# Order of transposes, squares and a small product around matmuls in halves, in a two-layer graph network on one core

## The chip, the core and the metric

The kernel runs on one core of a Trainium2 chip. The metric is the device time of one execution in microseconds (us). The core has five engines that matter here: TensorE (PE in the profile; its weight loads are PEld), VectorE (DVE), ScalarE (ACT), GpSimd (POOL) and SyncE (SP), which here issues nearly all transfers. Each works through its own list of instructions in order and waits for the others through semaphores.

## The reference

For each of 16 batches there are 1024 nodes with 128 features (`x`) and a 1024 x 1024 matrix `adj`. A first network adds a gathered, degree-scaled and weighted sum to `x` and normalises each node. A second network has four layers with both directions of the matrix, each normalised by the root of its sums of squares. All of it is in float32.

```python
def _L0_gnn_ref(embeddings, adjacency_matrix, cost_matrix, W, b):
    degree = adjacency_matrix.sum(axis=-1)[:, :, None]
    sum_neighbors = jnp.einsum('bid,bij->bjd', embeddings, cost_matrix) / degree
    concatenated = jnp.concatenate([embeddings, sum_neighbors], axis=-1)
    return jax.nn.relu(jnp.einsum('bnk,dk->bnd', concatenated, W) + b)

def _l2norm(x, axis):
    n = jnp.sqrt(jnp.sum(x * x, axis=axis, keepdims=True))
    return x / jnp.maximum(n, EPS)

def _layer(nodes, adj, ws, bs, wd, bd, wn, bn, wu, bu):
    src_agg = jnp.einsum('bjv,bij->biv', nodes @ ws + bs, _l2norm(adj, 2))
    dst_agg = jnp.einsum('bjv,bji->biv', nodes @ wd + bd, _l2norm(adj, 1))
    upd = jnp.concatenate([src_agg, nodes @ wn + bn, dst_agg], axis=2)
    return jnp.tanh(upd @ wu + bu)
# four such layers with kept inputs concatenated, then:
x = _layernorm(x + _L0_gnn_ref(x, adj, adj, L0_gnn_W, L0_gnn_b), axis=-1)
x = _layernorm(x + _L1_gnn_ref(x, adj, ...), axis=-1)
```

## The kernel before

The kernel works through the batches in turn. In the layers of batch `b` it already prepares batch `n = b + 1`: its degrees, its sums of squares by rows and columns, its scaling, its first network (`first_gnn`) and the transposed matrix `at`. Layers are numbered from 0, so "layer two" of the change's name is layer 1 in the code.

`aggregate` multiplies messages with quarters of the matrix in a Winograd form: seven products in place of eight, with combined quarters `T` (of `a`) and `Q` (of `at`). Two matmuls, in the upper and the lower half of the array's columns, are issued as a pair. A dictionary of `hooks` says at which pair other engines' work (and a few small products) enter the instruction lists.

```python
def transpose_rows(st, q, at):
    h, o = divmod(q * QB * C, HW)
    n = QB // len(st)
    for j in range(0, NB, NJ):
        for i, piece in enumerate(st):
            c = slice(o + i * n * C, o + (i + 1) * n * C)
            nc.vector.transpose(
                at[h][:, j:j + NJ, c].rearrange("p j (k c) -> p j k c", c=C),
                piece.rearrange("p k (j c) -> p j k c", c=C)[:, j:j + NJ])
...
def combine(i, y, T):
    if i == 2:
        nc.vector.tensor_sub(T[2], y[1, 1], y[0, 1])
    elif i == 3:
        nc.vector.tensor_sub(T[3], T[2], y[0, 0])
    else:
        nc.vector.tensor_sub(T[4], y[1, 0], T[2])
...
def degree_of(a, state, i, engine=nc.scalar):          # ScalarE, sum of a row
    ...
    nc.scalar.activation(a[:, i, :], a[:, i, :], AF.Copy, accum_out=degree)

def squares_of_row(n, a, state, i):                     # ScalarE
    sq = two.tile([P, N], F32, tag="sq", ...)           # two buffers
    nc.scalar.activation(sq, a[:, i, :], AF.Square, accum_out=state["cols"][:, i:i + 1])
    state[i] = sq

def add_squares(b, state, i):                           # VectorE
    ...
    nc.vector.tensor_add(state["acc"], state["acc"], state[i])

def column_sums(b, state):                              # VectorE: transpose, then reduce to `part`
    column_reduce(b, state, column_transpose(b, state))

def inverses(b, state, first=0):
    cols = state["cols"]
    pc = small(f"pc{b}")
    by_halves(pc, fold, state["part"])                  # TensorE: the column sums' product
    own = ...
    nc.vector.tensor_mul(own, pc..., group...)
    nc.vector.reduce_sum(cols[:, NB:2 * NB]..., own..., axis=AX.X)
    root_inverses(cols, state["inv"], slice(first, 2 * NB))   # VectorE max, GpSimd power
```

In layer 0 of every batch but the first, the rest of `at` is transposed from rows that ScalarE has scaled. Quarter 0 of the rows arrives in two pieces, in the buffers `xa` and `acc`; quarter 1 in two pieces in `sq` buffers.

```python
def rows3():
    for q in (1, 0):
        transpose_rows(rows[q], q, at)
hooks = {0: rows3, 3: lambda: combine(4, y, T), 5: lambda: combine_1(yt), 7: lambda: combine(2, yt, Q),
         9: lambda: combine(3, yt, Q), 11: lambda: combine(4, yt, Q), 17: sums1, 28: first_addition}
aggregate(b, 0, feats, t, a, at, T, Q, f1, "row", hooks)
```

In layer 1, at fixed pairs of `aggregate`, reads of the accumulators (`m1_read`, `m3_half`, `m4_read`, `m2_and_half_of_m3`, `last_reads`) are issued as well, the last at pair 22; the layer ends with an addition on VectorE and a tanh on ScalarE:

```python
for i, pair in enumerate(zip(up, lo)):
    if i - 2 * n in events:
        events[i - 2 * n]()
    if i in hooks:
        hooks[i]()
    for o, x, y, start, stop in pair:
        nc.tensor.matmul(o, x, y, start=start, stop=stop)
nc.vector.tensor_add(e0, e0, Z0)
squash(l, 0, e0, fT)
```

Then `messages` of layer 2 begins, with VectorE additions of the products `pt`; behind the first of them `factors` takes the result of `inverses`, and sends the column factors through memory to `cinv`, by which VectorE scales the next matrix (`a<-a,cinv`).

Of the kernel before, what the change touches and what calls it, by code (L numbers as in the profile page):

```python
# [23 lines left out]
def adj_resnorm_kernel(ctx: ExitStack, tc: tile.TileContext, x, adj, w0, b0, layers, out):  # L24
# [35 lines left out]
    NB = N // P  # L60
# [8 lines left out]
    NJ = NB // 2  # L69
# [107 lines left out]
    def small(name, shape=(K,)):  # L177
        return ps_s.tile([P, *shape], F32, tag="small", name=name)

    def by_halves(out, x, y, start=True, stop=True):  # L180

        for s in (slice(V, P), slice(V)):
            nc.tensor.matmul(out[s], x[:, s], y, start=start, stop=stop)  # L183
# [53 lines left out]
    def begin_sums(b):  # L237
        cols = two.tile([P, 3 * NB], F32, tag="cols", name=f"cols{b}")
        inv = two.tile([P, C], F32, tag="inv", name=f"inv{b}")
        nc.gpsimd.memset(inv[:, 3 * NB:], 0.0)  # L240
        return {"cols": cols, "inv": inv}
# [22 lines left out]
    def column_sums(b, state):  # L264

        column_reduce(b, state, column_transpose(b, state))

    def column_transpose(b, state):
        tr = two.tile([P, N], F32, tag="sq", name=f"acct{b}")
        nc.vector.transpose(tr, state["acc"])  # L270
        return tr

    def column_reduce(b, state, tr):
        part = two.tile([P, K], F32, tag="part", name=f"part{b}")
        nc.vector.reduce_sum(part, tr.rearrange("p (k r) -> p k r", r=C), axis=AX.X)
        state["part"] = part
# [16 lines left out]
# [4 lines that stand above are left out]
        by_halves(pc, fold, state["part"])  # L297
        own = one.tile([P, NH, G, BPH], F32, tag="own", name=f"own{b}")
        nc.vector.tensor_mul(own, pc.rearrange("p (h g k) -> p h g k", h=NH, g=G),
                             group[:, None, :, None].to_broadcast([P, NH, G, BPH]))  # L300
        nc.vector.reduce_sum(cols[:, NB:2 * NB].rearrange("p (h k) -> p h k", h=NH),
                             own.rearrange("p h g k -> p h k g"), axis=AX.X)
        root_inverses(cols, state["inv"], slice(first, 2 * NB))

    def root_inverses(cols, inv, s):
        nc.vector.tensor_scalar_max(cols[:, s], cols[:, s], NORM_EPS * NORM_EPS)
        nc.gpsimd.tensor_tensor(inv[:, s], cols[:, s], mhalf[:, s], ALU.pow)
# [115 lines left out]
    def summed(name, tag):  # L423
        return one.tile([P, K, C], F32, tag=tag, name=name)
# [127 lines left out]
    def scale_rows(st, q, rinv):  # L552
        n = QB // len(st)
        for k in range(QB):
            row = st[k // n][:, k % n]
            nc.scalar.activation(row, row, AF.Copy, scale=rinv[:, q * QB + k:q * QB + k + 1])

    def transpose_rows(st, q, at):
        h, o = divmod(q * QB * C, HW)
        n = QB // len(st)  # L560
        for j in range(0, NB, NJ):
            for i, piece in enumerate(st):
                c = slice(o + i * n * C, o + (i + 1) * n * C)
                nc.vector.transpose(  # L564
                    at[h][:, j:j + NJ, c].rearrange("p j (k c) -> p j k c", c=C),
                    piece.rearrange("p k (j c) -> p j k c", c=C)[:, j:j + NJ])
# [4 lines left out]
    def quarters(a):  # L571
        return {(j, h): a[:, j * NJ:(j + 1) * NJ, half(h)] for j in range(2) for h in range(NH)}

    def quarters_t(at):
        return {(j, h): at[h][:, j * NJ:(j + 1) * NJ] for j in range(2) for h in range(NH)}

    def combined(b, kind):

        return {i: one.tile([P, NJ, HW], F32, tag=f"{kind}{i}", name=f"{kind}{i}_{b}") for i in (2, 3, 4)}

    def combine_1(y):

        nc.vector.tensor_sub(y[0, 1], y[0, 1], y[0, 0])  # L583
# [8 lines that stand above are left out]
# [203 lines left out]
    FIRST, LAST, ALL = range(BPH), range(BPH, NB), range(NB)  # L795
# [32 lines left out]
    Q = combined(0, "Q")  # L828
# [166 lines left out]
    for b in range(B):  # L995
        nxt = b + 1 < B
        n = b + 1
        y, yt = quarters(a), quarters_t(at)
        st = {}
# [4 lines left out]
        if b == 0:  # L1004
# [25 lines left out]
            def fold_and_scale(l, q):  # L1030
                fold_begin(l, fetched[l])
                scale_rows(rows[q], q, rinv)
# [16 lines left out]
            def folded(l, part):  # L1049
                return lambda *_: part(l, fetched[l])  # L1050

            hooks = {4: lambda *_: inverses(0, st0, NB), 5: folded(2, fold_begin), 6: rows0, 7: cinv0,
                     8: folded(2, fold_end), 9: lambda *_: fold_and_scale(3, 0), 11: second0, 12: folded(3, fold_end),
                     14: lambda *_: scale_rows(rows[1], 1, rinv), 18: first0, 26: sums0}
            T = combined(0, "T")
# [4 lines left out]
        else:  # L1060
            w = {}
            if nxt:
                w["a"] = load(n)
                st = begin_sums(n)
            t = messages(b, 0, feats, wm)
            wm = message_weights(b, 1)
            Q = combined(b, "Q")
# [12 lines left out]
            def first_addition(st=st):  # L1080
                if nxt:
                    add_squares(n, st, 1)

            hooks = {0: rows3, 3: lambda: combine(4, y, T), 5: lambda: combine_1(yt), 7: lambda: combine(2, yt, Q),
                     9: lambda: combine(3, yt, Q), 11: lambda: combine(4, yt, Q), 17: sums1, 28: first_addition}
# [9 lines left out]
        def sums_of(*rows, of=(), engine=nc.scalar, add=()):  # L1095

            def issue():
                for i in of:
                    degree_of(a2, st, i, engine)
                for i in rows:  # L1100
                    squares_of_row(n, a2, st, i)
                for i in add:
                    add_squares(n, st, i)
            return issue

        hooks = {}
        if b == 0:
            hooks = {0: sums_of(0, 1, add=(1,)), 1: lambda: combine(2, yt, Q), 2: sums_of(2, 3, add=(2, 3)),
                     3: lambda: combine(3, yt, Q), 4: sums_of(4, 5, of=(0, 1), add=(4, 5)), 5: lambda: combine(4, y, T),
                     11: sums_of(of=(2, 3)), 13: sums_of(6, 7, of=(4,)), 15: sums_of(of=(5,)),  # L1110
                     18: lambda: combine(4, yt, Q), 19: sums_of(of=(6, 7), add=(6, 7)), 27: lambda: column_sums(n, st)}
            st = begin_sums(n)
        else:
            nm = f"1_{b - 1}"
            w = {"ys": summed(f"y{nm}", "xa")}
            sums_of_next = {}
            if nxt:
                sums_of_next = {1: sums_of(2, 3, add=(2,)), 2: sums_of(of=(2, 3, 4, 5)), 8: sums_of(4), 10: sums_of(add=(3,)),
                                12: sums_of(5, add=(4,)), 15: sums_of(6, add=(5,)), 19: sums_of(7, add=(6,)),
                                20: sums_of(of=(6,)), 21: sums_of(add=(7,)), 23: sums_of(of=(7,)),  # L1120
                                24: lambda: column_sums(n, st), 29: lambda: inverses(n, st)}

            def begin1(w=w, nm=nm):
                norm_spread(w["ys"], f4, KS)
                w["s"] = norm_sum(w["ys"], KS, nm, back)

            def centre1(w=w, nm=nm):
                w["sq"] = norm_centre(w["ys"], w["s"], KS, nm)
                if nxt:
                    w["xs"] = load_spread(n)  # L1130

            def squares1(w=w, nm=nm):
                w["v"] = norm_squares(w["sq"], KS, nm)

            def rstd1(w=w, nm=nm):
                w["r"] = norm_rstd(w["v"], KS, nm)

            hooks = {0: begin1, 11: centre1, 14: squares1, 18: rstd1, **sums_of_next}
        aggregate(b, 1, feats, t, a, at, T, Q, f23, "row", hooks)
        if b:  # L1140
            second_norm, xs2 = w, w.get("xs")


        feats = [(f1, 1), (f23, 0)]
# [42 lines left out]
        hooks, between = {4: end1} if b else {}, {}  # L1187
        if nxt:
            scales = [lambda: scale(0, 1), lambda: scale(NJ, 1), lambda: scale(0, 0), lambda: scale(NJ, 0)]
            if b == 0:  # L1190
                between = {1: inverses3, 3: factors}
                hooks = {1: load_xn, 5: factors_of_rows, 7: start3, 18: factors_gathered,
                         **dict(zip((10, 12, 14, 16), scales))}
                quarters_at = (20, 22, 25)
            else:
                between = {0: factors, 1: end1_and_load}
                hooks = {2: factors_of_rows, **dict(zip((4, 5, 7, 9), scales)), 10: factors_gathered, 16: start3}
# [12 lines left out]
        hooks, between = {}, {}  # L1210
        if nxt:
# [64 lines left out]
            hooks = {0: squares0, 7: rstd0, 10: rows0, 14: end0, 18: quarters0, 23: rows1, 27: rows2}  # L1276
        else:
# [14 lines left out]
            hooks = {30: residual_last, 31: transpose_last}  # L1292
# [5 lines left out]
        if nxt:  # L1298
# [4 lines left out]
            T = w["T"]  # L1303
# [52 lines left out]
```

## Time and profile before

| what | value |
|---|---|
| time, median of 3 runs | 2435.02 us (2433.85 to 2435.8) |
| span of the profiled run | 2438.5 us |
| TensorE busy | 2415.8 us, 99% |
| TensorE weight loads busy | 1058.5 us, 43% |
| VectorE busy | 1909.6 us, 78% |
| ScalarE busy | 957.1 us, 39% |
| matmul of 128x512 (one of a pair) | 592 to 597 ns |
| VectorE transpose of a split piece, 128x512 | 669 to 695 ns |
| VectorE addition of squares, 128x1024 | 1221 ns |
| ScalarE square of a row block, 128x1024 | 1048 ns |

A line of the timeline has the start in us from the span's start, the length in us, the engine, the line of the kernel, the operation and the tiles (out <- in); in brackets stands how long the engine was idle before it and what ended that. The list of waits gives the same idle times in sums. Matmuls overlap in the records, and their ends are modelled, so a stop of TensorE is best seen in the distance between starts.

### The profile page before, as it was taken

The page shows a single profiled execution, that of the slowest core. Times are in us where ns is not written, and L with a number is a line of the kernel's source. Part 1 is how long each engine was busy: PE and PEld are TensorE (multiplying, and loading weights), DVE is VectorE, ACT ScalarE, POOL GpSimd, SP SyncE. Part 2 cuts the span into 40 slices and gives each one's busy share as a digit, 9 for nine tenths or more (in the row PEclk, how much of TensorE's full clock was granted, in tenths as well). Part 3 has the DMA queues.
Part 4 walks back from the last instruction along what each step waited for, and adds up shares of the span by engine and source line. Part 5 has one row for each costly group of instructions (what it writes and reads, how often), then busy time and mean ns, then how long its engine had stood idle before and what let it go on. Part 6 is the DMA issues. An engine that isn't in the chain of part 4 may idle for free.

```text
span 2438.5 us, 34361 instructions
## 1 busy us (share of the span) xinstructions
PE 2415.8 (99%) x13245; PEld 1058.5 (43%) x13245; DVE 1909.6 (78%) x2495; ACT 957.1 (39%) x1794; POOL 287.1 (12%) x100
## 2 busy tenths in 40 slices
PE   8999999999999999999999999999999999999998
PEld 5433444444444344443444435444443444434433
DVE  5878878798787978869788787887878878798743
ACT  5415334263342624425244351533515334262321
POOL 4101111101111011110011110111100111101100
PEclk9999999999999999999999999999999999999999
DMA  9517254261633517245172352624427254261410
GB/s 207 108 48 150 53 113 90 66 135 44 135 80 73 116 44 156 62 88 101 45 160 59 83 106 58 142 59 99 94 63 140 52 121 93 63 126 44 96 24 9
DMA packets 365732, 219.92 MB, mean 90 GB/s; under 512 B 152769, under 2 KB 336833, under 8 KB 365569
## 3 DMA queue, kind: packets, MB, share of 16 engines
q1 hardware_dynamic: 364800, 215.36, 41.8%
q0 software_dynamic: 768, 2.36, 0.3%
q8 instruction: 105, 1.72, 0.3%
q14 instruction: 59, 0.48, 0.1%
HBM read 199.17 MB, written 18.46 MB: 89 GB/s over the span
## 4 chain that ended last, share of the span: by engine, by line
PE 78%; DMA 9%; DVE 8%; SPq 2%; issue 2%; ACT 1%; DVEq 0%; ACTq 0%; POOLq 0%
PE m L773 33%; PE z L773 20%; PE pt L183 14%; PE m_f L516 5%; DMA a<-in_adj_dram 5%; PE z_f L516 2%; PE pw L183 2%; DMA rows<-in_adj_dram 2%; DVE at L564 2%; SPq L549 2%; DMA rows_acc<-in_adj_dram 1%; DVE Q L587 1%; DVE at L583 1%; DVE T L591 1%; DMA raw<-in_L_gnn_ws_dram 1%
## 5 line engine op out<-in xcount | busy, mean ns | idle before, releaser
L773 PE MATMUL m<-Q,S 128*64 128x512 f32 x1008 | 445.4, 593 | 3.1 <-DVE Q L587 2.9
L387 POOL TENSOR_TENSOR rs<-ve,mhalf 128x32 f32<-128x32 f32 x30 | 205.2, 6839 | 1955.9 <-DVE ve L385 1955.9
L773 PE MATMUL m<-at,t 128*64 128x512 f32 x1008 | 395.3, 594 | 0.3 <-DVE at L564 0.3
L773 PE MATMUL m<-T,S 128*64 128x512 f32 x1008 | 394.9, 593 | 0.0
L773 PE MATMUL m<-a,t 128*64 128x512 f32 x1008 | 392.8, 593 | 0.0
L607 DVE TENSOR_TENSOR t<-pt,wm 128x512 f32<-128x512 f32 x256 | 175.2, 689 | 159.6 <-PE pt L183 159.5
L773 PEld LDWEIGHTS m<-Q,S 128*64 128x64 f32 x1008 | 135.6, 137 | 275.2 <-issue 259.7
L773 PE MATMUL z<-Q,t 128*64 128x512 f32 x504 | 231.0, 597 | 2.0 <-DVE Q L591 2.0
L686 ACT COPY e<-m 64x512 f32<-64x512 f32 x63 | 36.6, 580 | 496.5 <-PE m L773 496.1
L773 PE MATMUL z<-a,t 128*64 128x512 f32 x504 | 231.2, 597 | 0.0
L773 PE MATMUL z<-a,S 128*64 128x512 f32 x504 | 227.1, 593 | 0.0
L773 PE MATMUL z<-at,S 128*64 128x512 f32 x504 | 226.7, 592 | 0.0
L773 PE MATMUL z<-at,t 128*64 128x512 f32 x504 | 226.6, 592 | 0.0
L183 PE MATMUL pt<-wm,f1T 128*64 128x256 f32 x1536 | 219.4, 380 | 0.0
L773 PEld LDWEIGHTS m<-T,S 128*64 128x64 f32 x1008 | 122.1, 137 | 130.1 <-issue 128.2
L773 PEld LDWEIGHTS m<-at,t 128*64 128x64 f32 x1008 | 119.8, 137 | 130.5 <-issue 127.0
L773 PEld LDWEIGHTS m<-a,t 128*64 128x64 f32 x1008 | 121.1, 137 | 122.8 <-issue 119.5
L773 PE MATMUL z<-T,t 128*64 128x512 f32 x384 | 172.8, 592 | 0.0
L345 DVE TENSOR_TENSOR a<-a,cinv 128x512 f32<-128x512 f32 x250 | 154.2, 691 | 12.8 <-DMA cinv<-dr 9.1
L183 PE MATMUL pt<-wm,f23T 128*64 128x256 f32 x1024 | 160.5, 379 | 0.0
L253 ACT ACTIVATE sq<-a 128x1024 f32<-128x1024 f32 x120 | 125.7, 1048 | 69.6 <-DVE acc L262 61.5
L183 PEld LDWEIGHTS pt<-wm,f1T 128*64 128x64 f32 x1536 | 121.7, 137 | 58.4 <-ACT f1T L786 12.0
(238 smaller groups left out, 4278.1 us busy)
## 6 DMA issues: line engine op xcount, KB each, us to landing
a<-in_adj_dram SPq DMA_DIRECT2D x120, 512.0 KB, 11.3
a<-in_adj_dram SPq DMA_DIRECT2D x240, 128.0 KB, 4.4
rows<-in_adj_dram SPq DMA_DIRECT2D x240, 64.0 KB, 3.0
wm<-wsave SPq DMA_DIRECT2D x16, 512.0 KB, 4.7
xn<-in_x_dram SPq DMA_DIRECT2D x124, 64.0 KB, 2.0
wm<-wsave SPq DMA_DIRECT2D x31, 256.0 KB, 3.7
xs<-in_x_dram SPq DMA_DIRECT2D x60, 128.0 KB, 3.6
cinv<-dr SPq DMA_DIRECT2D x30, 256.0 KB, 5.3
```

The costliest lines, as they stand in the source:

```text
L183: nc.tensor.matmul(out[s], x[:, s], y, start=start, stop=stop)
L253: nc.scalar.activation(sq, a[:, i, :], AF.Square, accum_out=state["cols"][:, i:i + 1])
L345: engine.tensor_mul(a[:, i, s], a[:, i, s], cinv[:, s])
L387: nc.gpsimd.tensor_tensor(rstd, ve, mhalf[:, :n], ALU.pow)
L516: nc.tensor.matmul(o, x_, y_, start=start, stop=stop)
L549: queue.dma_start(piece[g * C:(g + 1) * C, :, h * P:(h + 1) * P], v[h, g, :, i * n:(i + 1) * n])
L564: nc.vector.transpose(at[h][:, j:j + NJ, c].rearrange("p j (k c) -> p j k c", c=C), piece.rearrange("p k (j c) -> p j k c", c=C)[:, j:j + NJ])
L583: nc.vector.tensor_sub(y[0, 1], y[0, 1], y[0, 0])
L587: nc.vector.tensor_sub(T[2], y[1, 1], y[0, 1])
L607: nc.vector.tensor_add(t[j][:, o:o + 2].rearrange("p k a v c -> p k (a v c)"), pt, wm[:, 0][:, None, :].to_broadcast([P, 2, 2 * P]))
L686: nc.scalar.copy(e0[high], A[high])
L773: nc.tensor.matmul(o, x, y, start=start, stop=stop)
```

## The change

Four things are done, and no operation is added or taken away. First, `transpose_rows` goes through a split quarter of rows piece by piece, so that both transposes of the first piece stand ahead of those of the second. Second, in every middle batch the small product of the column sums (`inverses`) is issued behind the last matmul of layer 1 instead of ahead of its last pair. Third, squares and their additions for the next matrix take other places in layer 1 of the middle batches. Fourth, in layer 1 of the first batch the degrees of the first four row blocks come early, those of the last four late, and the last two additions come behind the last reads of the accumulators. The aim is that TensorE does not have to wait for VectorE's and ScalarE's side work.

```diff
     def transpose_rows(st, q, at):
         h, o = divmod(q * QB * C, HW)
         n = QB // len(st)
-        for j in range(0, NB, NJ):
-            for i, piece in enumerate(st):
+        for i, piece in enumerate(st):
+            for j in range(0, NB, NJ):
                 c = slice(o + i * n * C, o + (i + 1) * n * C)
                 nc.vector.transpose(
...
         if b == 0:
-            hooks = {0: sums_of(0, 1, add=(1,)), 1: lambda: combine(2, yt, Q), 2: sums_of(2, 3, add=(2, 3)),
-                     3: lambda: combine(3, yt, Q), 4: sums_of(4, 5, of=(0, 1), add=(4, 5)), 5: lambda: combine(4, y, T),
-                     11: sums_of(of=(2, 3)), 13: sums_of(6, 7, of=(4,)), 15: sums_of(of=(5,)),
-                     18: lambda: combine(4, yt, Q), 19: sums_of(of=(6, 7), add=(6, 7)), 27: lambda: column_sums(n, st)}
+            hooks = {0: sums_of(0, 1, add=(1,)), 1: lambda: combine(2, yt, Q), 2: sums_of(of=FIRST),
+                     3: sums_of(2, 3, add=(2, 3)), 4: lambda: combine(3, yt, Q), 5: sums_of(4, 5, add=(4, 5)),
+                     6: lambda: combine(4, y, T), 13: sums_of(6, 7), 18: lambda: combine(4, yt, Q), 19: sums_of(of=LAST),
+                     22: sums_of(add=(6, 7)), 27: lambda: column_sums(n, st)}
...
                 sums_of_next = {1: sums_of(2, 3, add=(2,)), 2: sums_of(of=(2, 3, 4, 5)), 8: sums_of(4), 10: sums_of(add=(3,)),
-                                12: sums_of(5, add=(4,)), 15: sums_of(6, add=(5,)), 19: sums_of(7, add=(6,)),
-                                20: sums_of(of=(6,)), 21: sums_of(add=(7,)), 23: sums_of(of=(7,)),
-                                24: lambda: column_sums(n, st), 29: lambda: inverses(n, st)}
+                                12: sums_of(5, add=(4,)), 13: sums_of(6), 15: sums_of(add=(5,)),
+                                17: sums_of(add=(6,)), 19: sums_of(7), 20: sums_of(of=(6,)), 21: sums_of(add=(7,)),
+                                23: sums_of(of=(7,)), 24: lambda: column_sums(n, st)}
...
         aggregate(b, 1, feats, t, a, at, T, Q, f23, "row", hooks)
         if b:
             second_norm, xs2 = w, w.get("xs")
+            if nxt:
+                inverses(n, st)
```

`sums_of(rows, of, add)` issues the degrees `of`, the squares of `rows` and the additions `add`; `FIRST` and `LAST` are the first and last four row blocks.

## Prediction

> **What bounds the kernel now.** I read the page's first parts, then who waited for whom on TensorE, then the timeline of each place where TensorE's matmuls start late. The page first, the busy times and the row of the granted clock:
>
> ```profile
> PE 2415.8 (99%) x13245; PEld 1058.5 (43%) x13245; DVE 1909.6 (78%) x2495; ACT 957.1 (39%) x1794; POOL 287.1 (12%) x100
> ...
> PEclk9999999999999999999999999999999999999999
> ```
>
> TensorE is never without work for long, at full clock, and the change takes no matmul away. So the most the change can give is the time in which TensorE stands still. Who waited for whom, TensorE alone (total us, times, longest):
>
> ```profile
> PE m L773 <- DVE Q L587: 2.9, 7, 0.8
> PE z L773 <- DVE Q L591: 2.0, 1, 2.0
> ...
> PE pw L183 <- DVE e_f L508: 0.7, 1, 0.7
> PE pc L183 <- DVE part L275: 0.5, 1, 0.5
> ```
>
> These are too small, because a matmul's recorded length covers the start of a wait. I therefore went by starts: in an undisturbed stretch two matmuls (upper and lower half of the array) start together every 0.43 us. Over the whole trace I took every distance above that. Three families make up 14.5 us of the roughly 21 us; most of the rest is the start-up and about 1.3 us at the first batch's `pw`, which the change does not address.
>
> **Family A: before the product of the column sums (14 times).** TensorE's timeline at the end of layer 1:
>
> ```profile
> 561.57 0.59 PE L773 MATMUL z<-a,t 128*64 128x512 f32 x1
> 562.30 0.31 PE L183 MATMUL pc<-part,fold 128*64 128x32 f32 x4
> 562.41 0.62 PE L773 MATMUL z<-Q,t 128*64 128x512 f32 x1
> ```
>
> The four small matmuls cost 0.11 us (562.30 to 562.41), but they start at 562.30 instead of 562.00. VectorE's reduction `part` starts at 560.93, lasts 1.22 and ends at 562.15. So 0.30 us is lost, in 13 of 14 batches, and 0.67 in one: 4.6 us.
>
> **Family B: before `m<-Q,S` in layer 0 (11 of 15 batches).** VectorE and then TensorE:
>
> ```profile
> 1559.93 0.67 DVE L564 STREAM_TRANSPOSE at<-rows_xa 128x512 f32<-128x512 f32 x1
> 1561.30 0.71 DVE L564 STREAM_TRANSPOSE at<-rows_acc 128x512 f32<-128x512 f32 x1 [0.70 <-ACT rows_acc L556]
> 1561.94 0.67 DVE L564 STREAM_TRANSPOSE at<-rows_xa 128x512 f32<-128x512 f32 x1
> ```
> ```profile
> 1568.76 0.59 PE L773 MATMUL z<-a,t 128*64 128x512 f32 x1
> 1569.96 0.64 PE L773 MATMUL m<-Q,S 128*64 128x512 f32 x1 [0.61 <-DVE Q L587]
> ```
>
> A transpose of the second piece (`rows_acc`, scaled last by ScalarE) stands between the two of the first piece and waits for it. After it VectorE works without a gap to `Q`, and TensorE starts 0.06 us after `Q` is done. In the four batches where `rows_acc` was ready, TensorE does not stop.
>
> **Family C: once, in layer 1 of the first batch.** TensorE waits from 106.87 to 109.49 for `Q[4]`, and then runs slowly. The windows' columns are length, then busy time (and number) of PE, PEld, DVE, ACT, POOL, then the clock:
>
> ```profile
> 106.90:109.50 2.60, 0.58 (x6) 0.01 (x2) 2.59 (x3) 1.72 (x4) 0.00 (x0) 1.00 0.00 0
> 109.50:112.80 3.30, 3.30 (x8) 0.92 (x10) 3.20 (x4) 0.22 (x1) 0.00 (x0) 0.52 0.00 0
> ```
>
> Pairs then start 0.85 us apart, four times, before 0.43 returns. The last eight pairs should have ended at 106.87 + 9 x 0.43 = 110.73; the next product starts at 114.67. The loss is 3.9 us.
>
> **What the Trainium skill says.** "TensorE: Matmul & The Clock Gate", section "What's actually happening", says that the array's clock falls to half after an idle window of about 3.4 us and needs a busy window to return. The trace agrees in kind: clock 0.52 after the stop, though the stop was 2.2 us beyond the rhythm. So removing one stop removes the slow stretch too. The same page, section "Architectural detail: the array is 16× 32×32, not 1× 128×128", says that ScalarE and VectorE take their work strictly in order: this is family B (the ready `rows_xa` transpose waits behind `rows_acc`) and the cause of C below. "Perfetto Trace Analysis", section "Identifying the Most-Contended Engine", calls matmul busy share a bad measure of headroom; here 99% busy hides even part of the stops, as shown.
>
> **The change part by part.** Instruction counts stay what they were, except that a few semaphore waits move. SyncE's order is unchanged, so no transfer is moved by program order.
>
> *Transposes piece by piece (B).* The order becomes xa, xa, acc, acc. Transposes follow one another every 0.59 us, so the wait shrinks by up to one of them. For the batch above: `rows_acc` is ready at 1561.27; two xa transposes begin at 1559.93 and 1560.53, acc at 1561.30 and 1561.9; the chain to `Q` starts at 1562.48 instead of 1563.12. Doing this for all 15 batches, VectorE is ahead by 0.28, 0.23, 0.35, 0.64, 0.64, 0.42, 0.61, 0.64, 0.21, 0.43 and 0.48 us where it had waited: 4.9 us. What the stops cost is the batch period (start of `pc` to start of `pc`) less 148.88, the period of a batch without them: 6.0 us. So 4.9 is saved and about 1.1 stays, nearly all in the batch at 963 us, whose wait was 1.46 us. The new order makes the first half of `at` complete one transpose later; in undisturbed batches its reader had 1.1 us in hand and keeps 0.5, so no new stop.
>
> *Product at the end of layer 1 (A).* `pc` goes behind the last pair, about 0.86 us later than TensorE wants it now, so `part` (562.15 or earlier) is there. All 4.6 us go. What it moves: on VectorE the last addition `e<-e,z` now comes ahead of the three small operations on `pc`, and is 0.47 us earlier. These three (0.19 + 0.21 + 0.17) end near 564.4 instead of 563.29, GpSimd's power (2.90) near 567.4 instead of 566.34, and the column factors land about 1.05 us later, 1.4 us later against TensorE. VectorE waits for GpSimd ahead of the second message addition; the fourth slips by 0.36 us against TensorE. Its readers start 1.3 us after the sums `S` they need, so it holds. The 16 scalings (9.72 us) shift by 1.05 us; behind them VectorE stood idle for 1.1 to 2.2 us (1.48 here) waiting for TensorE at the end of layer 2. The shift fits in that idle time, and the first batch, whose factors come 6 us later still, has no stop before `pw`.
>
> *Squares and additions, later batches.* Square 6 now stands ahead of ScalarE's copies `m4`, waits for VectorE's reduction (to 550.93) and ends near 552.1. Addition 6 fills VectorE's 0.57 us idle stretch ahead of `e<-e,m` and delays that by 0.7, but only addition 7 is left between it and the reads that follow. `part` comes about 0.4 us earlier. With `pc` moved, this is worth nothing more by itself.
>
> *First batch (C).* ScalarE did the degrees of rows 2 to 4 (98.21 to 101.35) and squares 6 and 7 ahead of the copies at 103.55 that let `e<-e,e` and then `Q[4]` go. Now four degrees lie at about 85 to 89, where ScalarE was idle for 4.80 us. Squares 6 and 7 wait for additions 4 and 5 (98.0, 99.33) and end at about 100.5; copies to 101.7; `e<-e,m` on VectorE as before, 101.56 to 102.25; copy, addition, then `Q[4]` from 103.65 to 105.9. TensorE wants it at 107.30: no stop, no slow clock, 3.9 us. But additions 6 and 7 (2.48 us) now stand behind the reads, so the last addition of the layer ends about 3.3 us after TensorE's last product, against 2.4 now. The small chain to the column factors slips with it, and `pw`, which waits for their result, may lose 0.4 us. Net 3.5.
>
> *Sum:* 4.9 + 4.6 + 3.5 = 13.0 us. 2435.0 - 13.0 = 2422.0 us.
>
> **The rivals.** First, *the later column factors become the wait*: for it speaks that every batch's scaling moves by over 1 us and VectorE is busy from there to the end of layer 2; against it the idle time of at least 1.1 us there and the several us that the combinations `T2` to `T4` are ahead of `first_gnn`. If half a microsecond per batch came back, the time would be 2429. Second, *the loads set layer 0*: `rows_acc` arrives by DMA and ScalarE waits 3.96 us and more for it, so if TensorE's time saved in layer 1 makes the arrival later against TensorE, B yields only half: 2424.5. The loads start when VectorE releases buffers in layer 3, and layer 3 keeps its place against TensorE, which speaks against. Third, *square 6 ahead of ScalarE's copies* delays the layer's end: 0.2 us in 14 batches would give 2425.
>
> **Range and chances.** All costs counted are in TensorE's own line, so a gain is nearly sure; TensorE's product time, over 2400 us, caps it at under 1%. Against a sum of 13, errors go mostly one way (new small stops), so the range is 2419 to 2428. Over 2% in either direction would need 49 us: chance 0.01 below, 0.005 above.
>
> **What would show it.** Right: no distance above 0.5 us before `pc`; `m<-Q,S` stops only near 955 us; clock 1.00 in layer 1 of the first batch and `Q[4]` before TensorE comes; TensorE's idle sum down by 13. Wrong: stops at products of layer 2 or `first_gnn`, a first-batch `pw` wait grown beyond 1 us more, or waits for `rows_acc` as long as before in spite of the order.

## The result, and the profile after

| what | before | after |
|---|---|---|
| time, median of 4 runs each | 2435.41 us (2433.85 to 2437.97) | 2424.47 us (2423.69 to 2425.38) |
| ratio after to before | | 0.9954, 95% interval 0.9937 to 0.9971 |
| span of the profiled run | 2438.5 us | 2421.9 us |

The changed kernel is faster by 10.9 us; the interval of the ratio allows 7.1 to 15.3 us (2435.4 times 0.0029 and 0.0063). 2422.0 us had been predicted, and 13.0 us of gain. The two spans differ by 16.6 us, but they are single executions. About 1.3 us of that lies in the start-up, which the change does not touch: TensorE's stop at the first `pa` alone was 1.1 us in one and 0.5 in the other, and a second profile of the kernel before had 2.0.

The page first, TensorE's row and the granted clock:

```profile
PE 2407.9 (99%) x13245; PEld 955.6 (39%) x13245; DVE 1904.8 (79%) x2495; ACT 958.5 (40%) x1794; POOL 273.5 (11%) x100
...
PEclk9999999999999999999999999999999999999999
```

Busy time fell by 7.9 us with the same 13245 matmuls, because busy time contained parts of the stops and the matmuls at half clock; the percentage still says 99. The weight loads' busy time fell by 103 us, but that brought next to no time: it is about 955 us in every kernel that has `pc` behind the last pair and 1054 or more in every other, and the changed kernel with `pc` put back, at 1054.5, is 0.7 us slower than the changed kernel. The lengths of the single loads sum to 1857 us after and 1859 before, so the loads only overlap more. The list of waits, TensorE alone, no longer names `Q` or `part`; of the lines shown before, only the wait of the first batch's `pw` is left (total us, times, longest):

```profile
PE pw L183 <- DVE e_f L508: 0.5, 1, 0.5
```

Measured by starts, as in the prediction, the distances over 0.5 us exceed the rhythm of 0.43 by 5.9 us in sum, against 20.8 before.

**Family A, end of layer 1.** TensorE's timeline in the same batch as before:

```profile
555.97 0.59 PE L773 MATMUL z<-a,t 128*64 128x512 f32 x1
556.39 0.26 PE L183 MATMUL pc<-part,fold 128*64 128x32 f32 x4
556.48 0.63 PE L183 MATMUL pt<-wm,f1T 128*64 128x256 f32 x4
```

The last matmul of the layer starts at 555.97, `pc` 0.42 us later, in the rhythm, and the messages follow 0.09 us behind. VectorE in the same stretch:

```profile
554.17 1.22 DVE L275 TENSOR_REDUCE part<-acct 128x32 f32<-128x1024 f32 x1
556.61 0.69 DVE L775 TENSOR_TENSOR e<-e,z 128x512 f32<-128x512 f32 x1 [1.22 <-PE z L773]
...
560.93 0.17 DVE L328 TENSOR_TENSOR cols<-cols,inv 128x8 f32<-128x8 f32 x1 [1.78 <-POOL inv L307]
```

`part` is ready at 555.39, a full microsecond ahead of `pc`. In the kernel before it ended at 562.15, where TensorE wanted to go on at 562.00 (VectorE's line of before):

```profile
560.93 1.22 DVE L275 TENSOR_REDUCE part<-acct 128x32 f32<-128x1024 f32 x1
```

The bracket of the line at L328 is the new wait that came with the move of `pc`: VectorE idles 1.78 us for GpSimd's power in every middle batch, where it was 0.42 before.

**Family B, layer 0.** VectorE first, then TensorE:

```profile
1547.03 1.26 DVE L564 STREAM_TRANSPOSE at<-rows_xa 128x512 f32<-128x512 f32 x2
1548.22 1.26 DVE L564 STREAM_TRANSPOSE at<-rows_acc 128x512 f32<-128x512 f32 x2
```

```profile
1555.85 0.59 PE L773 MATMUL z<-a,t 128*64 128x512 f32 x1
1556.28 0.60 PE L773 MATMUL m<-Q,S 128*64 128x512 f32 x1
```

The four transposes run without a gap, and `m<-Q,S` starts 0.43 us after the pair before it. In this execution no batch waited for `rows_acc` at all.

**Family C, first batch.** The windows that were shown for the kernel before (columns: length, busy time and number of PE, PEld, DVE, ACT, POOL, then the clock):

```profile
106.90:109.50 2.60, 2.60 (x16) 0.89 (x14) 2.57 (x3) 0.72 (x1) 0.00 (x0) 1.00 0.03 6
109.50:112.80 3.30, 3.30 (x34) 2.21 (x32) 3.23 (x5) 0.00 (x0) 0.00 (x0) 1.00 0.28 81
```

TensorE is busy through both, at clock 1.00.

### The profile page after: what moved, and what is told of

It reads as the page before. It is cut to its first block, busy times and chain, and to the rows that moved or that the text cites. A ratio compares the mean times of both kernels' runs of the same rounds, so it can differ in the third digit from the quotient of the medians.

```text
span 2421.9 us, 34377 instructions
## 1 busy us (share of the span) xinstructions
PE 2407.9 (99%) x13245; PEld 955.6 (39%) x13245; DVE 1904.8 (79%) x2495; ACT 958.5 (40%) x1794; POOL 273.5 (11%) x100
## 4 chain that ended last, share of the span: by engine, by line
PE 97%; DMA 1%; SPq 1%; DVE 0%; ACT 0%; issue 0%; POOLq 0%; DVEq 0%
PE m L773 44%; PE z L773 26%; PE pt L183 16%; PE m_f L516 5%; PE pw L183 2%; PE z_f L516 2%; DMA raw<-in_L_gnn_ws_dram 1%; PE z L652 1%; ACT Q L556 0%; SPq L549 0%; PE d L652 0%; DMA wsave<-wm 0%; DMA a<-in_adj_dram 0%; DMA raw<-in_L_gnn_wn_dram 0%; PE pv L183 0%
## 5 line engine op out<-in xcount | busy, mean ns | idle before, releaser
L387 POOL TENSOR_TENSOR rs<-ve,mhalf 128x32 f32<-128x32 f32 x30 | 191.6, 6385 | 1941.5 <-DVE ve L385 1941.5
L183 PE MATMUL pt<-wm,f1T 128*64 128x256 f32 x1536 | 213.3, 381 | 0.0
L345 DVE TENSOR_TENSOR a<-a,cinv 128x512 f32<-128x512 f32 x250 | 154.3, 694 | 27.8 <-DMA cinv<-dr 22.3
L183 PE MATMUL pt<-wm,f23T 128*64 128x256 f32 x1024 | 154.1, 379 | 0.0
L183 PE MATMUL pt<-wm,x_T 128*64 128x256 f32 x1024 | 135.5, 379 | 0.0
```

The lines of the kernel that those rows point to most:

```text
L345: engine.tensor_mul(a[:, i, s], a[:, i, s], cinv[:, s])
L387: nc.gpsimd.tensor_tensor(rstd, ve, mhalf[:, :n], ALU.pow)
```

## The experiments

A is the move of `pc` behind the last pair (before, the timelines show two pairs behind `pc`, where the text ahead of the prediction speaks of one), B the order of the transposes, C the first batch's hooks, and D the places of squares and additions in layer 1 of the middle batches.

Twelve runs were made, in four sets. The kernels of a set ran on one chip beside the kernel before, and the sets' chips differ. "Gain" is the median of before in that set less the kernel's own. The medians of before lie between 2437.64 and 2438.69 us, so gains of different sets compare to about 1 us; inside a set some tenths count where ranges do not overlap. One execution of the kernel before in set 4 took 3927.29 us at a granted clock of 0.609 and is not counted.

| set | kernel | time, us (range; runs) | before, us | gain | ratio, 95% interval |
|---|---|---|---|---|---|
| 1 | before, again | 2439.13 (2436.36–2441.18; 12) | 2438.69 | -0.4 | 0.9999 (0.9991–1.0007) |
| 1 | B alone | 2434.54 (2433.29–2436.43; 19) | 2438.69 | 4.2 | 0.9983 (0.9976–0.9990) |
| 1 | A alone | 2434.56 (2432.75–2435.85; 21) | 2438.69 | 4.1 | 0.9982 (0.9976–0.9989) |
| 1 | C alone | 2435.58 (2433.18–2439.30; 13) | 2438.69 | 3.1 | 0.9988 (0.9979–0.9996) |
| 2 | changed, again | 2425.10 (2425.00–2426.41; 4) | 2438.61 | 13.5 | 0.9945 (0.9928–0.9962) |
| 2 | D alone | 2433.70 (2431.89–2435.41; 11) | 2438.61 | 4.9 | 0.9982 (0.9973–0.9991) |
| 2 | changed without A | 2425.76 (2425.20–2425.89; 4) | 2438.61 | 12.9 | 0.9946 (0.9931–0.9960) |
| 2 | changed, weights later | 2424.08 (2423.22–2424.99; 4) | 2438.61 | 14.5 | 0.9939 (0.9924–0.9954) |
| 3 | changed without D | 2425.81 (2424.58–2426.17; 4) | 2437.64 | 11.8 | 0.9947 (0.9932–0.9962) |
| 3 | changed without A and D | 2430.25 (2429.27–2432.69; 5) | 2437.64 | 7.4 | 0.9965 (0.9951–0.9979) |
| 3 | changed without B | 2430.21 (2428.42–2431.60; 5) | 2437.64 | 7.4 | 0.9966 (0.9953–0.9979) |
| 4 | changed, late copies | 2428.42 (2428.04–2429.77; 5) | 2438.25 | 9.8 | 0.9963 (0.9948–0.9978) |

The theory for A, B and C was the prediction's: each part removes stops of TensorE's own line, and the gains add. The rivals were that one part brings it all, that the part called worthless (D) is not, and that the slow clock is what costs in C.

### The kernel before, once more

No edit: this shows what two measurements of one kernel differ by, and what of a profile stays from execution to execution.

> The kernel before, unchanged, profiled once more. The first profile had waits of VectorE for rows_acc of 4.8 us in sum and a span 16.6 us above that of the changed kernel, while the timed runs differ by 10.9 us. Theory 1 (the landing of rows_acc varies from execution to execution, and the first profile was a bad draw): the period of a batch is again 148.87 us where rows_acc is in time, but the waits sum to 1 to 3.5 us, and the span is 2433 to 2436. Theory 2 (the waits are a fixed property of the program, and the timed runs differ for another reason): waits of 4.5 to 5.1 us in the same batches, span near 2438.

The ratio is 0.9999 (0.9991 to 1.0007), so times of this set hold to about 2 us. Neither theory came true. The first profile was no bad draw: the waits are longer still, and the span is 2439.4 us. But they do not lie in the same batches either: the longest had been 1.5 us at 963 us, and is now 1.7 us at 1262. Two places of the profile differ from the first one of the same kernel. The waits for `rows_acc` are now 12 with 5.7 us (9 with 4.6 in the first profile). And the first batch's stop comes with another sequel, TensorE's timeline:

```profile
109.01 0.64 PE L773 MATMUL z<-Q,t 128*64 128x512 f32 x1 [2.03 <-DVE Q L591]
...
114.40 0.65 PE L183 MATMUL pt<-wm,f23T 128*64 128x256 f32 x4 [1.30 <-ACT f23T L786]
```

The stop of the first line is there as before, but the clock stays whole in the window behind it:

```profile
109.00:112.40 3.40, 3.39 (x16) 1.20 (x18) 3.30 (x4) 0.29 (x1) 0.00 (x0) 1.00 0.00 2
```

That gains TensorE almost nothing: it comes sooner to the messages and stops there for `f23T`, the second line above. From the first `z<-T,t` of the layer to the first own product of layer 2 (`z<-f1T,wown`) it took 17.66 us; with the slow clock in the first profile, 17.83.

### The parts alone

For B alone, the transposes:

```diff
-        for j in range(0, NB, NJ):
-            for i, piece in enumerate(st):
+        for i, piece in enumerate(st):
+            for j in range(0, NB, NJ):
```

> Only the transposes piece by piece. Theory 1: no stop before m<-Q,S but in a batch with a wait over 0.6 us; the stops before pc and in the first batch's layer 1 stay; 2 to 4.5 us less than before. Theory 2 (a fixed 4.9 us): 4.5 to 5.5 us less. Rival (the wait for rows_acc only moves, to the first reader of at): less than 1 us less, with stops before m<-at,t.

It gained 4.2 us. One wait for `rows_acc` remains, of 1.1 us; the list of waits, VectorE:

```profile
DVE at L564 <- ACT rows_acc L556: 1.1, 1, 1.1
```

The period of a batch (start of `pc` to start of `pc`) is 148.87 us in most middle batches, that of the undisturbed batches before; three were longer, by up to 1.2.

For A alone, the small product:

```diff
-                                 24: lambda: column_sums(n, st), 29: lambda: inverses(n, st)}
+                                 24: lambda: column_sums(n, st)}
...
+            if nxt:
+                inverses(n, st)
```

> Only the product pc behind the last pair of layer 1, squares and additions as before. Theory: no stop before pc, 14 x 0.30 to 0.36 plus 0.37 once: 4.6 to 5.3 us less. Rival (the later column factors give it back in layer 2): 0 to 3 us less, with stops in first_gnn.

It gained 4.1 us (the interval allows 2.7 to 5.9), a little under the 4.6 expected, and far from all being given back in layer 2. The waits for `rows_acc` are as in the kernel before (6.0 us in 11), so this part does nothing to B's family.

For C alone, the first batch's hooks:

```diff
-                     3: lambda: combine(3, yt, Q), 4: sums_of(4, 5, of=(0, 1), add=(4, 5)), 5: lambda: combine(4, y, T),
-                     11: sums_of(of=(2, 3)), 13: sums_of(6, 7, of=(4,)), 15: sums_of(of=(5,)),
-                     18: lambda: combine(4, yt, Q), 19: sums_of(of=(6, 7), add=(6, 7)), 27: lambda: column_sums(n, st)}
+                     3: sums_of(2, 3, add=(2, 3)), 4: lambda: combine(3, yt, Q), 5: sums_of(4, 5, add=(4, 5)),
+                     6: lambda: combine(4, y, T), 13: sums_of(6, 7), 18: lambda: combine(4, yt, Q), 19: sums_of(of=LAST),
+                     22: sums_of(add=(6, 7)), 27: lambda: column_sums(n, st)}
```

> Only the first batch's order of degrees, squares and additions in layer 1. Theory: 3.9 us less there (no stop at Q[4], clock 1.00 behind it), of which 0.1 to 0.4 comes back as a stop at the messages of layer 2 or at pw: 3.5 to 3.9 us less. Rival (the stop's slow clock is not due to it): 2.2 us less.

It gained 3.1 us (the interval allows 1.0 to 5.1), so the times alone do not decide between the theory's 3.5 to 3.9 and the rival's 2.2. In the trace the stretch from `z<-T,t` to the first own product of layer 2 is 14.11 us, against 17.66 in the kernel before of the same set: 3.55 us, as the theory had it.

The three gains add up to 11.4 us. The changed kernel, run again in the next set, gained 13.5.

### The changed kernel again, D alone, and the change without A

> The changed kernel, unchanged, on this chip. Theory: its batches run at TensorE's own pace (period 148.52 us again, no wait for rows_acc unless one is over 0.6 us), so its times spread less than those of the kernel before (4.5 us over 55 runs); 11 to 16 us less than before. Rival (the first profile was a good draw): periods of 148.9 and more in several batches.

It gained 13.5 us, and TensorE's distances over 0.5 us exceed the rhythm by 6.8 us, against 21.9 in the kernel before of the first set. Nearly every middle batch took 148.52 us, of which only some 0.1 us lies above the rhythm; two took 148.58 and 149.06. The second is a wait for `rows_acc` that came back in spite of the order (VectorE's timeline):

```profile
1250.85 1.26 DVE L564 STREAM_TRANSPOSE at<-rows_xa 128x512 f32<-128x512 f32 x2
1252.53 1.30 DVE L564 STREAM_TRANSPOSE at<-rows_acc 128x512 f32<-128x512 f32 x2 [0.42 <-ACT rows_acc L556]
```

D alone takes from the change only the middle batches' squares, and leaves `pc` at pair 29:

```diff
-                                12: sums_of(5, add=(4,)), 15: sums_of(6, add=(5,)), 19: sums_of(7, add=(6,)),
-                                20: sums_of(of=(6,)), 21: sums_of(add=(7,)), 23: sums_of(of=(7,)),
-                                24: lambda: column_sums(n, st), 29: lambda: inverses(n, st)}
+                                12: sums_of(5, add=(4,)), 13: sums_of(6), 15: sums_of(add=(5,)),
+                                17: sums_of(add=(6,)), 19: sums_of(7), 20: sums_of(of=(6,)), 21: sums_of(add=(7,)),
+                                23: sums_of(of=(7,)), 24: lambda: column_sums(n, st), 29: lambda: inverses(n, st)}
```

> Only the squares and additions of the middle batches in their new order, pc still ahead of the last pair. Theory (the two are substitutes): part is ready 0.4 us earlier, so pc finds it ready, and the stops before pc vanish though pc was not moved: 4 to 4.8 us less than before, as with pc alone moved (4.1). Rival (as the prediction had it: worth nothing by itself, only moving pc helps): 0 to 1 us less, stops before pc of 0.2 to 0.3 us.

It gained 4.9 us, as much as the move of `pc`. TensorE and then VectorE at the end of layer 1:

```profile
559.47 0.59 PE L773 MATMUL z<-a,t 128*64 128x512 f32 x1
559.90 0.31 PE L183 MATMUL pc<-part,fold 128*64 128x32 f32 x4
560.01 0.62 PE L773 MATMUL z<-Q,t 128*64 128x512 f32 x1
```

```profile
558.53 1.22 DVE L275 TENSOR_REDUCE part<-acct 128x32 f32<-128x1024 f32 x1
```

`part` ends at 559.75, and `pc`, still with two pairs behind it, starts at 559.90 in the rhythm: 0.43 us after the pair before it, where it was 0.73 in the kernel before. That holds in 13 of the 14 batches (0.70 in one), and with A alone in all 14. The squares' new order alone removes nearly all of family A.

The other side of the same question is the changed kernel with `pc` put back to pair 29:

```diff
-                                23: sums_of(of=(7,)), 24: lambda: column_sums(n, st)}
+                                23: sums_of(of=(7,)), 24: lambda: column_sums(n, st), 29: lambda: inverses(n, st)}
...
-            if nxt:
-                inverses(n, st)
```

> The changed kernel with pc back ahead of the last pair of layer 1. Theory (substitutes): period 148.5 to 148.6 us, the same time as the changed kernel within 1 us, and VectorE's wait for the column factors shorter by about 1 us per batch. Rival (moving pc is needed): 4 us more than the changed kernel.

It lost 0.7 us to the changed kernel in its set, with ranges that overlap. Its usual period is 148.57 us against 148.52: 0.05 in each of 14 batches is the same 0.7. VectorE's wait for GpSimd is back at 0.42 us a batch, as in the kernel before, and the shorter wait buys nothing.

### Without D, and without both

Without D, `pc` stays behind the last pair and the squares take their old order (the diff of D, reversed, without its pair 29). Without both, `pc` goes back to pair 29 too.

> The changed kernel with the squares and additions of the middle batches in their old order (pc still behind the last pair). Theory (either of the two is enough): period 148.5 to 148.6 us, no stop before pc or the messages of layer 2, the changed kernel's time within 1 us. Rival (the order of the squares is what counts): 3 us or more above the changed kernel.

> The changed kernel with both undone, so only the transposes and the first batch changed. Theory: the stop before pc is back, period 148.87 us, 14 x 0.35 = 4.9 us above the changed kernel. Rival (the stops are filled by slack elsewhere once the others are gone): within 2 us of it.

Without D the period was 148.52 us in most batches (148.57 to 148.78 in three, and 149.53 in one with a wait for `rows_acc`), and the gain was 11.8. Without both it was 148.87 again in most batches and the gain 7.4, and TensorE's stop before `pc` is back in all 14 batches, 0.72 to 0.73 us from start to start:

```profile
556.93 0.59 PE L773 MATMUL z<-a,t 128*64 128x512 f32 x1
557.66 0.31 PE L183 MATMUL pc<-part,fold 128*64 128x32 f32 x4
```

Within this set the second undoing costs 4.4 us, and the period gives (148.87 - 148.52) x 14 = 4.9 us. So A and D are substitutes: undoing either costs under 2 us, undoing both costs the whole of family A.

### Without B

The changed kernel with the old order of the transposes.

> The changed kernel with the old order of transposes. Theory: stops before m<-Q,S in 9 or more batches, with waits for rows_acc of 2 to 6 us in sum, 3 to 6 us above the changed kernel, and times that spread by over 2 us again. Rival (rows_acc lands earlier in the changed kernel, so its order no longer matters): within 1.5 us of it.

The gain fell from 13.5 to 7.4, and the median rose by 5.1 above that of the changed kernel; the sets differ, so I call B worth 5 to 6 us here. TensorE stops before `m<-Q,S` in 13 batches, and nine have a wait of VectorE that the list of waits shows:

```profile
DVE at L564 <- ACT rows_acc L556: 3.9, 9, 1.3
```

Over all executions, the old order had 9 to 12 waits and 3.9 to 6.0 us, except in D alone, which had 5 and 2.1. The new order had 0 to 3 waits and at most 2.6 us. Which batches wait changes from execution to execution, because the landing does. In nearly every middle batch the load of `rows_acc` (eight transfers) is begun 2.0 us before TensorE's first own product of layer 0 (`z<-x_T,wown`), and its last part lands 4.7 to 6.8 us after that product's start. But the late landings are not spread evenly: over the 14 profiles, one more than 6.0 us behind came in the batch at 1248 to 1262 us in ten, in the batch at 952 to 963 us in four, and in no other middle batch. Why there, no run tells.

### Late copies in the first batch

C moves degrees and squares away from ahead of ScalarE's copies, and also moves the last two additions behind the reads. Here the degrees and squares go back, and the additions stay moved:

```diff
-                     6: lambda: combine(4, y, T), 13: sums_of(6, 7), 18: lambda: combine(4, yt, Q), 19: sums_of(of=LAST),
-                     22: sums_of(add=(6, 7)), 27: lambda: column_sums(n, st)}
+                     11: sums_of(of=(2, 3)), 13: sums_of(6, 7, of=(4,)), 15: sums_of(of=(5,)),
+                     18: lambda: combine(4, yt, Q), 19: sums_of(of=(6, 7)), 22: sums_of(add=(6, 7)), 27: lambda: column_sums(n, st)}
```

> This is the changed kernel whose first batch takes back the old places of the degrees, of the squares and of ScalarE's copies (the late order), with one thing kept from the new order: the additions 6 and 7 stay at pair 22, ahead of where the late squares and copies are. Theory (the late copies and squares themselves set the end of layer one in the first batch, neither the order of the additions nor the clock): the stop of about 2.2 us ahead of the first z<-Q,t comes back; the second stop stays, at one of the first products that read f23T; from the first z<-T,t to the first own product of layer two it takes 17.2 to 17.9 us, against 14.1 in the changed kernel, and the time is 3 to 4 us above the changed kernel's. Rival one (the additions that stood behind the late copies made the second stop): the second stop is gone, only the first one is back: 16.3 us for the same stretch, and 2.2 us of time. Rival two (the slow clock makes the second loss): the stretch is 16.3 us where the granted clock is 1.00 and 17.8 where a slice of it falls to about half.

The stretch took 17.22 us, and the time is 3.3 us above the changed kernel's (3.7 by gains). Both rivals are refuted by it: the second stop came with the additions moved, and at whole clock. TensorE's timeline shows both stops:

```profile
109.10 0.64 PE L773 MATMUL z<-Q,t 128*64 128x512 f32 x1 [2.04 <-DVE Q L591]
...
116.27 0.31 PE L183 MATMUL pc<-part,fold 128*64 128x32 f32 x4
116.41 0.63 PE L183 MATMUL pt<-wm,f1T 128*64 128x256 f32 x4
117.61 0.65 PE L183 MATMUL pt<-wm,f23T 128*64 128x256 f32 x4 [0.58 <-ACT f23T L786]
```

The first stop is the old one. The second has moved from the first group of products with `f23T` to the first group behind `pc`, which needs the other half. VectorE's chain explains it: it waits 4.19 us for ScalarE's late copy, and from 106.04 on it works without a gap through `Q[4]`, the reads, the additions, `part` and `e<-e,z` (to 116.81), which the last `f23T` needs. Its first line:

```profile
106.04 0.69 DVE L711 TENSOR_TENSOR e<-e,e 64x512 f32<-64x512 f32 x1 [4.19 <-ACT e L695]
```

The same line of the changed kernel, where the copy came early:

```profile
101.62 0.69 DVE L711 TENSOR_TENSOR e<-e,e 64x512 f32<-64x512 f32 x1 [0.68 <-ACT e L695]
```

The order within that chain decides which product waits, and about 0.4 us (17.66 to 17.22), not whether one does. The move of the additions alone was not run. Behind the first stop the clock was 1.00:

```profile
109.10:112.50 3.40, 3.40 (x16) 1.20 (x18) 3.23 (x5) 1.34 (x2) 0.00 (x0) 1.00 0.00 0
```

### The column factors of the first batch, sooner

The prediction left the first batch's `pw` aside as 1.3 us. It waits for a chain that goes through memory: SyncE writes `dr` and reads `cinv` back. SyncE's timeline in the changed kernel:

```profile
117.59 0.34 SPq L174 DMA_DIRECT2D wm<-wsave  x1
118.27 0.34 SPq L333 DMA_DIRECT2D dr<-invt  x1
121.36 0.92 SPq L339 DMA_DIRECT2D cinv<-dr  x2
```

The write stands behind a load of 512 KB of message weights, and the read comes 3.09 us after the write. TensorE's line at `pw` in the same trace:

```profile
158.61 1.08 PE L183 MATMUL pw<-e_f,w0T 128*64 128x512 f32 x4 [0.47 <-DVE e_f L508]
```

In this edit, for the first batch alone, ScalarE issues that load later:

```diff
-        wm = message_weights(b, 3)
+        if b:
+            wm = message_weights(b, 3)
+        else:
+            def later():
+                tile_ = message_tile("wm4_0")
+                nc.scalar.dma_start(tile_[:, :CHUNKS[3] + 1], wsave[3])
+            ...
+            hooks[19] = later
```

> The changed kernel, with the first batch's load of the last layer's message weights (512 KB) issued later by ScalarE, not by SyncE ahead of the column factors' small transfer. Theory (that load holds up the small transfer: 3.1 us from issue to the next issue, 1.5 us in other batches): the factors land 1 to 1.5 us earlier in the first batch and the stop of 1.05 us at pw shrinks to 0.2 or less: 0.8 to 1 us less than the changed kernel, in the trace. Rival (the transfer takes 3 us there anyway): no change.

SyncE, and then TensorE's `pw` (this execution's start-up took 1.6 us longer than the one above, `pc` starting at 114.45 and not 112.86, so only distances compare):

```profile
119.85 0.34 SPq L333 DMA_DIRECT2D dr<-invt  x1
121.42 0.94 SPq L339 DMA_DIRECT2D cinv<-dr  x2
```

```profile
157.83 1.89 PE L183 MATMUL pw<-x_T,w0T 128*64 128x512 f32 x8
159.55 1.89 PE L183 MATMUL pw<-e_f,w0T 128*64 128x512 f32 x8
```

The read follows the write by 1.57 us, and the stop at `pw` is gone: from the first own product of layer 2 to the messages of layer 3 it takes 43.03 us instead of 44.26. The median is 1.0 us below the changed kernel's. The two ranges of four runs just miss each other (2424.99 and 2425.00), and the two intervals against before overlap, so the trace shows this better than the times do. Its median is the lowest of all here. The edit takes the load out of the way altogether; whether the write had waited for its place behind the load or for the memory that the load kept busy, it does not tell.

## Why the prediction was right, and where not

The predicted 2422.0 us lies 2.5 below the measured 2424.47, and the measured time is inside the range of 2419 to 2428. The gain of 13.0 stands between the 10.9 of that comparison and the 13.5 of the second. By its own steps:

| step | predicted, us | part alone | undone in the changed kernel |
|---|---|---|---|
| A, stops before `pc` | 4.6 | 4.1 (D alone 4.9) | 4.4 to 6.1, both A and D undone |
| B, stops before `m<-Q,S` | 4.9 | 4.2 | 5.1 to 6.1 |
| C, first batch | 3.5 | 3.1 | 3.3 to 3.7 |
| sum | 13.0 | 11.4 | 12.8 to 15.9; whole change 13.5 |

In the last column the lower and the higher figure differ by how the sets are compared (medians inside or across a set, or gains).

**A was right in size and mechanism, but put down to one of two edits that each suffice.** The prediction said of the squares' order: "With `pc` moved, this is worth nothing more by itself." As a statement on the whole change that held to within 0.7 us by medians and 1.7 by gains. What the prediction missed stood in its own text: "`part` comes about 0.4 us earlier" is more than the 0.30 us by which `pc` was late. D alone showed that this is enough. In the batch shown, `part` starts 0.93 us ahead of the third-last pair with the new order (554.79 and 555.72, changed without A) and 0.63 ahead with the old one (555.43 and 556.06, changed without D): 0.30 us earlier, which is just the stop. With the old order `part` ended 0.15 us after TensorE's due time for `pc` (562.15 and 562.00 before), with the new one 0.15 ahead of it (559.75 and 559.90 in D alone). Undoing A alone therefore gave 0.7 us where family A is worth over 4.

**What A moves went as worked out.** VectorE's wait for GpSimd grew to 1.78 us in 14 batches, and its waits for `cinv` to 22.3 us; its idle time before the last addition of layer 2 shrank from 1.1–2.2 us to 0–0.9; TensorE did not stop there. The first rival, later factors as the new wait, did not happen. The third, square 6 ahead of the copies, did not either: the period of 148.52 us is below that of an undisturbed batch before.

**B was right in mechanism, but what stays was read from one execution.** The prediction had "about 1.1 stays, nearly all in the batch at 963 us". In the changed kernel's two profiles nothing and then one wait of 0.42 us in the batch at 1252 us stayed. Over all eight profiles with the new order it was 0 to 2.6 us, most of it in the batch near 1250 us and once at 958 us. So the batch at 963 us was one of two in which the load can land late, and in which of them it does changes from execution to execution. The second rival (loads later against TensorE, half of the worth) is refuted by the change without B.

**C was right in size, and its second half had the wrong cause.** The prediction took the loss for a stop of 2.2 us and a slow clock behind it, and said from the Trainium skill ("TensorE: Matmul & The Clock Gate", section "What's actually happening") that "removing one stop removes the slow stretch too". Six executions had the stop (the kernel before twice, A, B and D alone, late copies), and only the first of them a clock near half. The others took 17.22 to 17.66 us over the stretch, it took 17.83, and the changed kernel 14.11. So the clock was worth about 0.2 us, and the second part of the loss is VectorE's chain behind ScalarE's late copy, which stops TensorE at `f23T` when it comes there sooner. The page gives an idle window of about 3.4 us for the fall, and says that the window runs freely; that fits a fall in some executions alone, but here it fell once in six after a stop of 2.6 us from start to start, shorter than that window. The 0.4 us deducted for `pw` did not come: its two stops were 0.63 and 0.43 us with the change, and 0.84 and 0.43 (1.05 and 0.43 in the second execution) without. A stop of about 0.2 us at `f23T` came in its place. That the net of 3.5 comes so close to the 3.55 to 3.7 us measured over the stretch is therefore partly luck. The late copies, which C removes, stood behind both halves of the loss, so that the wrong cause of the second half did no harm, and a stop that was not foreseen took the place of the one that was.

What stays open: why the landing of `rows_acc` scatters by 2 us, and why it is late in just two batches; and why the first comparison gives 10.9 us and the second 13.5. Each lies in the other's interval, and the difference is on the side of the kernel before: its median of four runs there, 2435.41, is 2.2 to 3.3 us below those of the four sets, while the changed kernel's two medians are 0.6 apart.

## What to carry to other kernels

Where two edits of a change shorten the same wait, compare each one's slack with the wait before giving one of them the credit, and undo both, not one, to learn what the wait is worth. A slow clock behind a stop is not yet a loss: follow the other engine's queue to the next point where they meet, and see whether TensorE would have waited there anyway. And read a wait for a load from several executions: here one profile showed it in 9 batches and the next of the same kernel in 12, with the longest elsewhere.

## What the runs showed of the hardware

- The fall of the clock after the same stop of about 2.6 us from start to start came in one of six executions (0.52 in the window shown with the prediction, 1.00 in the other five). In that one the half clock lasted from 109.66 to 113.08 us.
- The first batch's small write to memory (`dr`) landed 2.95 us after its issue with the load of 512 KB just ahead, and 1.43 us with that load later; 1.42 is also the usual value of the other batches. Over the 13 profiles with the load just ahead it was 2.89 to 3.21 us. "DMA: Bandwidth & Descriptors" of the Trainium skill, section "Latency and other measured facts", says that memory latency rises to about 2 us under load and that this makes up most of a small transfer's fixed cost; the trace agrees in direction, but no run here separates that latency from a place behind the load. The next batch's write took 3.24 us in the changed kernel and 3.03 with the load later, though no such load stood just ahead; what held it up was not followed.
- A load begun at the same point of the program (2.0 us before the first own product of layer 0) was complete 6.7 to 8.8 us later in the middle batches of 14 profiles, and only in two of these batches later than 8.0.
